# Loading the node features in four pieces instead of two, and running the first layer norm by the same pieces

## The chip, the cores and the metric

The kernel runs on one NeuronCore of a Trainium2 chip, in one launch. The metric is the device time of one execution in microseconds (us); lower is better. Five engines work beside each other, each in the order of its own instruction queue: TensorE (PE) multiplies matrices, VectorE (DVE) does elementwise work and reductions, ScalarE (ACT) applies functions and copies, GpSimd (POOL) does small side work, SyncE (SP) issues transfers. ACT and POOL can issue transfers too. An engine waits for another, or for a transfer, through semaphores.

## What is computed

There are 3327 nodes with 64 features each (`x`) and a dense 3327 x 3327 adjacency matrix (`adj`). Two graph layers follow each other, both of the form "normalise, rectify, aggregate over neighbours, add to x":

```python
def _layernorm(x, axis=-1, eps=1e-5):
    m = jnp.mean(x, axis=axis, keepdims=True)
    v = jnp.var(x, axis=axis, keepdims=True)
    return (x - m) / jnp.sqrt(v + eps)

# --- layer 0: hyperbolic attention over the neighbours ---
h = jnp.maximum(_layernorm(x, axis=-1), 0.0)
x = x + _L0_gnn_ref(h, adj, L0_gnn_r, L0_gnn_w_att, L0_gnn_b_att)
#   left, right = logmap0(h) @ w_att halves
#   adj_att[i,j] = sigmoid(left[i] + right[j] + b) * adj[i,j]
#   support[i]   = sum_j adj_att[i,j] * logmap(h[i], h[j])
#   out          = proj(expmap(h, support))
# --- layer 1: each row's last 100 neighbours, weighted by powers of 1/2 ---
h = jnp.maximum(_layernorm(x, axis=-1), 0.0)
x = x + _L1_gnn_ref(h, adj, L1_gnn_weight, L1_gnn_bias)
```

The change touches only the first layer norm, at the very start: the load of `x`, the row sums, the centred values, their squares and their positive parts.

## The kernel before

The nodes are padded to 3328 = 26 blocks of 128, and a tile holds one node of each block per partition: `x_sb` is 128 partitions x 26 blocks x 64 features, 32-bit. One block of one partition is a run of 256 bytes in memory.

**The opening (lines 452 to 768).** `x_sb` is filled by two transfers of 13 blocks each, the first issued by SP (line 455), the second by ACT (line 456). SP then issues four loads of adjacency tiles (`ad`, line 617, 512 KB each); POOL issues seven small loads, among them `r_c` (line 460) and `w_lr` (line 471), and makes constants. For each half of the blocks, VectorE sums the rows (`m`, line 715) and subtracts the mean (`d`, line 716). ScalarE then forms three tiles: `sq` = d squared (line 717), `rl` = the positive part of d (line 718), `sr` = rl squared (line 719). A second loop over the halves reduces `sq` and `sr` on VectorE to the row quantities `v` and `rs` (lines 721 and 722):

```python
    node_halves = (slice(0, 13), slice(13, NB))
    for hs in node_halves:
        n = hs.stop - hs.start
        V.tensor_reduce(m[:, hs], x_sb[:, hs], AX.X, ALU.add)
        V.scalar_tensor_tensor(d[:, hs], wide(m[:, hs], n), -1.0 / D, x_sb[:, hs], op0=ALU.mult, op1=ALU.add)
        A.activation(sq[:, hs], d[:, hs], AF.Square)
        A.activation(rl[:, hs], d[:, hs], AF.Relu)
        A.activation(sr[:, hs], rl[:, hs], AF.Square)
    for hs in node_halves:
        V.tensor_reduce(v[:, hs], sq[:, hs], AX.X, ALU.add)
        V.tensor_reduce(rs[:, hs], sr[:, hs], AX.X, ALU.add)
```

After `rs` of the second half VectorE runs a long chain of small instructions on all 26 blocks at once (lines 749 to 781): scaling, an inverse square root by Newton steps, and interleaved with it the preparation of constants from `r_c` and `w_lr` (lines 729 to 743; the cast to `w_h` at line 741 needs `w_lr`). ScalarE loads another function table at line 725 and takes logarithms (lines 799 and 800). Then TensorE transposes the features, and the main loop starts.

**The main loop (lines 1194 to 1244).** It goes over four strips of target nodes and over 26 blocks of source nodes; each round loads an `ad` tile, makes a 0/1 `mask` (line 623), counts edges by matmul (lines 634, 635), forms pair products by matmul (lines 673, 674), passes them through ScalarE (lines 1211, 1212, 656) and VectorE (lines 661, 666), and sums by matmul into `po` (line 683). The per-node work of a finished strip is slipped between rounds. Layer 1 follows (lines 1252 to 1327).

**Order.** The instructions of PE, DVE and ACT from line 692 on stand in the order in which the code writes them (`manual_schedule` over these three engines); SP and POOL have queues of their own. A general version of the kernel stands behind a flag and isn't taken for these inputs.

Of the kernel before, what the change touches and what calls it, by code (L numbers as in the profile page):

```python
# [24 lines left out]
NB = 26  # L25
# [420 lines left out]
def fast(ctx, tc, x, adj_t, r, w_att, b_att, weight, bias, out, flag):  # L446

    nc = tc.nc
# [3 lines left out]
    x_sb = const.tile([P, NB, D], F32, name="x_sb")  # L452
    xv = x.rearrange("(t p) d -> p t d", p=P)
    node_halves = (slice(0, 13), slice(13, NB))
    nc.sync.dma_start(x_sb[:, :13], xv[:, :13])
    nc.scalar.dma_start(x_sb[:, 13:], xv[:, 13:])

    def across(src, n, name):
        t = const.tile([P, n], F32, name=name)
# [66 lines left out]
    def wide(t, n):  # L526
        return t[:, :, None].to_broadcast([P, n, D])
# [182 lines left out]
    m, rs = (small(n) for n in ("m", "rs"))  # L710
    v2, y2, t2 = (pre.tile([P, 2, NB], F32, name=n) for n in ("v2", "y2", "t2"))
    v, y = v2[:, 0], y2[:, 0]
    for hs in node_halves:
        n = hs.stop - hs.start
        V.tensor_reduce(m[:, hs], x_sb[:, hs], AX.X, ALU.add)
        V.scalar_tensor_tensor(d[:, hs], wide(m[:, hs], n), -1.0 / D, x_sb[:, hs], op0=ALU.mult, op1=ALU.add)
# [3 lines that stand above are left out]
# [610 lines left out]
@with_exitstack  # L1330
def gnn_kernel(
    ctx: ExitStack,
    tc: tile.TileContext,
    x: bass.AP,
    adj_t: bass.AP,
    r: bass.AP,
    w_att: bass.AP,
    b_att: bass.AP,
    weight: bass.AP,
    bias: bass.AP,  # L1340
    out: bass.AP,
):
    keep = ctx.enter_context(tc.tile_pool(name="keep", bufs=1))
    flag = keep.tile([1, 1], I32, name="flag")
    args = (x, adj_t, r, w_att, b_att, weight, bias, out)
    with ExitStack() as inner:
        fast(inner, tc, *args, flag)
    cond = tc.nc.values_load(flag)
    with tc.If(cond > 0):
        with ExitStack() as inner:  # L1350
            general(inner, tc, *args)
# [28 lines left out]
```

## Time and profile before

| what | value |
|---|---|
| time, median of 8 runs | 419.79 us |
| lowest and highest of the 8 | 417.69 and 421.76 us |
| the profiled execution, its own time | 417.8 us |
| its span, first to last instruction | 415.9 us |
| busy: DVE, ACT, PE, POOL | 91%, 87%, 86%, 27% of the span |
| mean granted TensorE clock | 0.972 of full speed |

The profile is of one execution. Its own time is 1.9 us more than its span, and 2.0 us below the median of the eight runs. All times inside the kernel below are counted from the start of that span. A row of the timeline gives the start, the time taken, the engine, the line, the operation, the tile written and the tiles read, the shape, and in brackets how long the engine had been idle and what ended that. A row of the chain of waits gives a start and a duration on the path that ended last, followed back from the last instruction. A row of the table of stretches gives for each engine its busy time, then the granted clock, the mean busy share of the DMA engines and the GB/s that they moved.

### The profile page before, as it was taken

Reading aid. Unit: us, or ns where it says so; the run is one execution under the profiler, and the core shown is the slowest. Engines: PE = TensorE matmul, PEld = TensorE weight load, DVE = VectorE, ACT = ScalarE, POOL = GpSimd, SP = SyncE. Lnnn points to the kernel's source line nnn. Section 1 sums busy time; section 2 is a strip of 40 time slices with the busy share of each in tenths; the row PEclk is TensorE's granted clock in tenths of the full one; section 3 lists DMA queues with packets and bytes.
Section 4 is the critical chain, followed back from the end, with each engine's and each line's share of the span. In section 5 each row is a group of like instructions: output and inputs, shape, how many; then the busy total and the mean of one; then the engine's idle time right before and its main releaser. Section 6 shows DMA issues by size and latency. Waiting matters only on the chain.

```text
span 415.9 us, 4717 instructions
## 1 busy us (share of the span) xinstructions
PE 359.0 (86%) x1460; PEld 152.9 (37%) x1460; DVE 377.7 (91%) x559; ACT 363.1 (87%) x409; POOL 112.9 (27%) x224
## 2 busy tenths in 40 slices
PE   0085999999997999999999899999787999899793
PEld 0053333333332333333333444444332333344353
DVE  4999999999999989999999998899999899898841
ACT  3587889999998999999999999999996999788820
POOL 7030000000000153950250073810505184452400
PEclk9998899999999899999999999999998999999987
DMA  8313545454548335544445454444543320000012
GB/s 184 157 40 116 178 129 155 134 177 134 176 129 249 102 112 171 154 127 145 139 123 154 122 153 125 141 125 142 172 145 103 110 92 0 2 0 1 2 25 65
DMA packets 23298, 48.99 MB, mean 118 GB/s; under 512 B 8789, under 2 KB 9245, under 8 KB 23265
## 3 DMA queue, kind: packets, MB, share of 16 engines
q1 hardware_dynamic: 20993, 47.66, 37.8%
q0 software_dynamic: 464, 0.49, 0.7%
q10 hardware_dynamic: 1808, 0.46, 0.6%
q8 instruction: 13, 0.21, 0.2%
q14 instruction: 20, 0.16, 0.1%
HBM read 46.40 MB, written 0.87 MB: 114 GB/s over the span
## 4 chain that ended last, share of the span: by engine, by line
DVE 43%; ACT 25%; PE 16%; issue 11%; POOL 3%; DMA 1%; DVEq 0%; POOLq 0%; ACTq 0%
DVE sg L666 12%; DVE sg L661 11%; ACT sg L656 7%; ACT pq L1211 7%; PE po L683 6%; DVE behind_lo L649 3%; DVE wt L1268 3%; ACT pq L1212 3%; DVE behind_hi L649 2%; ACT behind_hi L645 2%; ACT behind_lo L645 2%; PE pq L674 2%; PE pc L634 2%; PE pw L1280 2%; PE pq L673 2%
## 5 line engine op out<-in xcount | busy, mean ns | idle before, releaser
L683 PE MATMUL po<-sg,hw 128*65 128x512 f32 (+1 forms) x364 | 160.7, 565 | 0.4 <-DVE st L958 0.4
L666 DVE SCALAR_TENSOR_TENSOR sg<-pq,sg 128x1024 f32<-128x1024 f32 (+1 forms) x91 | 103.6, 1139 | 6.4 <-ACT pq L1212 5.8
L661 DVE SCALAR_TENSOR_TENSOR sg<-sg,ad 128x1024 f32<-128x1024 f32 (+1 forms) x91 | 103.9, 1142 | 0.1
L656 ACT ACTIVATE sg<-left_b,right 128x1024 f32<-128x1024 f32 (+2 forms) x103 | 99.5, 979 | 0.0
L1211 ACT ACTIVATE pq<-pq 128x1024 f32<-128x1024 f32 (+1 forms) x90 | 86.2, 958 | 2.8 <-PE pq L674 2.7
L1212 ACT ACTIVATE pq<-pq 128x1024 f32<-128x1024 f32 (+1 forms) x90 | 85.3, 947 | 2.9
L683 PEld LDWEIGHTS po<-sg,hw 128*65 128x65 f32 x364 | 49.5, 138 | 70.4 <-issue 56.6
L634 PE MATMUL pc<-mask,ca 128*128 128x512 bf16 (+1 forms) x175 | 64.2, 367 | 12.7 <-DVE behind_hi L649 4.5
L673 PE MATMUL pq<-iu,ju 71*128 71x512 f16 (+1 forms) x182 | 68.4, 376 | 1.4 <-ACT jz L797 0.8
L635 PE MATMUL pc<-mask,cb 128*128 128x512 bf16 (+1 forms) x182 | 65.4, 370 | 2.0 <-ACT behind_lo L645 1.7
L674 PE MATMUL pq<-iz,jz 128*128 128x512 f16 (+1 forms) x182 | 66.8, 374 | 0.0
L623 DVE TENSOR_SCALAR mask<-ad 128x1024 bf16<-128x1024 f32 (+1 forms) x91 | 58.9, 647 | 0.0
L1280 PE MATMUL pw<-wt,s 128*128 128x512 bf16 (+1 forms) x154 | 34.2, 376 | 4.0 <-DVE s L1135 2.2
L635 PEld LDWEIGHTS <-cb 128*128 128x128 bf16 x182 | 17.9, 98 | 53.6 <-issue 42.0
L1030 POOL TENSOR_TENSOR dots<-dots,ih 128x8 f32<-128x8 f32 (+1 forms) x3 | 2.2, 719 | 128.3 <-DVE dots L1050 128.3
L634 PEld LDWEIGHTS <-ca 128*128 128x128 bf16 x175 | 17.1, 98 | 29.6 <-issue 17.7
L1280 PEld LDWEIGHTS <-s 128*128 128x128 f16 x182 | 18.0, 101 | 24.0 <-issue 4.8
L673 PEld LDWEIGHTS <-ju 71*128 71x128 f16 x182 | 18.1, 99 | 23.0 <-DVE sg L666 4.3
L674 PEld LDWEIGHTS <-jz 128*128 128x128 f16 x182 | 18.3, 100 | 19.7 <-issue 2.8
L645 ACT ACTIVATE behind_lo<-pc 128x1024 uint8<-128x1024 f32 (+2 forms) x29 | 24.9, 859 | 0.0
L645 ACT ACTIVATE behind_hi<-pc 128x1024 uint8<-128x1024 f32 (+2 forms) x23 | 19.8, 859 | 5.1 <-PE pc L635 5.0
L1285 POOL TENSOR_TENSOR x_sb<-x_sb,bias_b 128x256 f32<-128x256 f32 (+1 forms) x6 | 9.9, 1657 | 51.3 <-DVE w L1119 45.7
(317 smaller groups left out, 364.5 us busy)
## 6 DMA issues: line engine op xcount, KB each, us to landing
ad<-in_adj_t SPq DMA_DIRECT2D x65, 512.0 KB, 3.5
ad<-in_adj_t SPq DMA_DIRECT2D x26, 384.0 KB, 3.1
out<-o SPq DMA_DIRECT2D x6, 128.0 KB, 1.9
left_b<-left_d SPq DMA_DIRECT2D x1, 512.0 KB, 4.3
x_sb<-in_x ACTq DMA_DIRECT2D x1, 416.0 KB, 5.6
x_sb<-in_x SPq DMA_DIRECT2D x1, 416.0 KB
left_b<-left_d SPq DMA_DIRECT2D x1, 384.0 KB
jz<-iz POOLq DMA_DIRECT2D x2, 128.0 KB, 2.6
```

The source lines that it names most:

```text
L634: T.matmul(S.pc[:, f0:f1], ca, S.before[:, f0:f1], start=False, stop=True, skip_group_check=True)
L635: T.matmul(S.pc[:, f0:f1], cb, now[:, f0:f1], start=S.first, stop=True, skip_group_check=True)
L645: A.activation(kept, S.pc[:, : S.F], AF.Relu, scale=128.0 if j in JD else 1.0)
L656: A.activation(part(n, sg, j), S.left[:, : S.F], AF.Tanh, bias=right[:, j : j + 1], scale=0.5)
L661: V.scalar_tensor_tensor(sg, sg, 1.0, ad_of.pop(n)[:, :w], op0=ALU.add, op1=ALU.mult)
L666: V.scalar_tensor_tensor(sg, pq_of.pop(n)[:, :w], WD, sg, op0=ALU.add, op1=ALU.mult)
L673: T.matmul(part(n, pq, j, f0, f1), ju[:KB, j, :], S.iu[:, f0:f1], start=True, stop=False)
L674: T.matmul(part(n, pq, j, f0, f1), jz[:, j, :], S.iz[:, f0:f1], start=False, stop=True)
L683: T.matmul(S.po[: D + 1, f0:f1], hw[:, j, :], part(n, sg_of[n], j, f0, f1), start=j == NB - 1, stop=j == 0)
L1211: A.activation(pq, pq, AF.Gelu, scale=-WG / QS)
L1212: A.activation(pq, pq, AF.Gelu, scale=WH)
L1280: T.matmul(pw[n], s2[:, j].rearrange("p c d -> p (c d)"), wt[:, f0:f1].bitcast(BF16), start=j == order[0], stop=j == NB - 1)
```

## The change

The two transfers of 13 blocks become four of 7, 6, 7 and 6 blocks: SP issues the first and the third, ACT the second and the fourth. The first loop of the layer norm (`m`, `d`, `sq`, `rl`, `sr`) goes over these four pieces. The second loop (`v`, `rs`) still goes over the two halves; pieces one and two are the first half, three and four the second.

```diff
@@ -452,8 +452,9 @@
     x_sb = const.tile([P, NB, D], F32, name="x_sb")
     xv = x.rearrange("(t p) d -> p t d", p=P)
     node_halves = (slice(0, 13), slice(13, NB))
-    nc.sync.dma_start(x_sb[:, :13], xv[:, :13])
-    nc.scalar.dma_start(x_sb[:, 13:], xv[:, 13:])
+    pieces = (slice(0, 7), slice(7, 13), slice(13, 20), slice(20, NB))
+    for n, part in enumerate(pieces):
+        (nc.scalar if n % 2 else nc.sync).dma_start(x_sb[:, part], xv[:, part])
@@ -710,7 +711,7 @@
     m, rs = (small(n) for n in ("m", "rs"))
     v2, y2, t2 = (pre.tile([P, 2, NB], F32, name=n) for n in ("v2", "y2", "t2"))
     v, y = v2[:, 0], y2[:, 0]
-    for hs in node_halves:
+    for hs in pieces:
         n = hs.stop - hs.start
         V.tensor_reduce(m[:, hs], x_sb[:, hs], AX.X, ALU.add)
         V.scalar_tensor_tensor(d[:, hs], wide(m[:, hs], n), -1.0 / D, x_sb[:, hs], op0=ALU.mult, op1=ALU.add)
```

## The prediction

> **What bounds the kernel now.** I read the page's chain of waits first, then that chain in order of time for the opening, then the timeline of VectorE there, and last the tables of DMA packets and of stretches for the load of x.
>
> The page's shares say what a microsecond is worth, and where:
>
> ```profile
> DVE 43%; ACT 25%; PE 16%; issue 11%; POOL 3%; DMA 1%; DVEq 0%; POOLq 0%; ACTq 0%
> ```
>
> DMA is 1% of the path; it is a single transfer, the first one. The chain for the first 14 us shows it and what comes behind it:
>
> ```profile
> 0.80 4.90 DMA x_sb<-in_x
> 5.72 1.03 DVE m L715
> 6.78 1.17 DVE d L716
> 7.96 0.90 ACT sq L717
> ...
> 10.58 0.79 ACT sq L717
> 11.36 0.80 ACT rl L718
> ...
> 12.18 0.91 ACT sr L719
> ...
> 13.11 1.02 DVE rs L722
> ```
>
> So the path is: wait for the first half of x until 5.70, two VectorE instructions on it, six ScalarE instructions in a row (7.96 to 13.09), then the last reduction at 13.11. From there the whole chain of small instructions hangs on that reduction. I call its start "the mark": whatever moves the mark moves all behind it. VectorE's own timeline shows how close it is to being the bound itself:
>
> ```profile
> 5.72 1.02 DVE L715 TENSOR_REDUCE m<-x_sb 128x13 f32<-128x832 f32 x1 [5.72 <-DMA x_sb<-in_x]
> 7.85 1.01 DVE L715 TENSOR_REDUCE m<-x_sb 128x13 f32<-128x832 f32 x1
> 9.89 1.01 DVE L721 TENSOR_REDUCE v<-sq 128x13 f32<-128x832 f32 x1
> 10.82 1.00 DVE L722 TENSOR_REDUCE rs<-sr 128x13 f32<-128x832 f32 x1
> 11.74 1.00 DVE L721 TENSOR_REDUCE v<-sq 128x13 f32<-128x832 f32 x1
> 13.11 1.02 DVE L722 TENSOR_REDUCE rs<-sr 128x13 f32<-128x832 f32 x1 [0.36 <-ACT sr L719]
> ```
>
> The two pairs m and d take 4.17 us (5.72 to 9.89), the next three reductions step by 0.93 and 0.92, and only 0.36 us of waiting for ScalarE is left before the mark.
>
> **The transfers.** What the SP queue (q1) had moved at 2.7 and at 3.2 us, packets of 256 bytes, and the stretches of one microsecond:
>
> ```profile
> q1 hardware_dynamic: 637, 0.16, 57.8%
> ```
> ```profile
> q1 hardware_dynamic: 1017, 0.26, 66.0%
> ```
> ```profile
> 1.75:2.75 1.00, 0.00 (x0) 0.00 (x0) 0.00 (x0) 0.85 (x1) 0.99 (x3) 1.00 0.76 177
> 2.75:3.75 1.00, 0.00 (x0) 0.00 (x0) 0.00 (x0) 0.00 (x0) 1.00 (x2) 1.00 1.19 271
> ```
>
> A half is 13 x 128 = 1664 packets. SP's half runs alone at first: until 2.7 the ACT queue moved nothing. SP's packets had all run by 4.85, and the wait ended at 5.70, so 0.85 us lie between the last packet and the landing. The ACT half had run by 6.0 and landed at 6.39 (issue at 0.79, 5.6 to landing): 0.4 us.
>
> The first piece of the new kernel is 7 x 128 = 896 packets, issued by the same engine at the same time. Between 637 at 2.7 and 1017 at 3.2 that count is reached at 3.04. With 0.85 to the landing it is there at 3.9, with 0.4 at 3.45. The late bound: ACT's shorter transfer may start earlier beside it, and then half of all bytes (426 kB) are through at 3.67 (177 kB until 2.75, 271 kB in the next microsecond), landing at 4.5. I take 3.9, because SP's own half has the 0.85. VectorE starts at 3.9 instead of 5.7.
>
> **VectorE after it.** Four pairs m and d instead of two. Rows near those sizes: the same two operations on 512 elements take 0.671 and 0.677 (lines 1117 and 1119), on 384 elements 0.543 and 0.558. For 448 elements that is 0.61 and 0.62. Four pairs are 2 x (0.61 + 0.62 + 0.54 + 0.56) = 4.66, less 0.04 overlap each as in the pairs of now: 4.50. The other way: two more reductions at a fixed part of 0.12 (1.014 at 832 against 0.671 at 512) and two more subtractions at 0.20 (0.677 at 512 against 0.558 at 384) on top of 4.17: 4.81. I take 4.65, 0.48 more than now. Then come 2.77 us for v, rs, v, and the mark is 7.42 us after VectorE's start, if neither ScalarE nor a transfer is later.
>
> ScalarE runs twelve instructions instead of six. Independent ones step by 0.51 at 512 elements and 0.20 at 128 (lines 804 to 808), so 0.46 at 448 and 0.41 at 384; `sr` waits some 0.11 more for `rl`, as now. Four pieces are 2 x (1.49 + 1.34) = 5.66, 0.6 more than now. It starts 1.29 after VectorE (0.61 + 0.62 and the gaps), and `sr` is done 7.05 after: 0.37 before VectorE gets to the mark. The 0.6 costs nothing as long as VectorE stays later; if VectorE's four pairs were free of added cost, ScalarE would set the mark at 7.07 instead.
>
> The third piece is needed at about 6.2, the fourth at 7.4. Today both halves have landed by 6.39, and the bytes are the same, so I charge no wait.
>
> **Sum.** The mark moves from 13.11 to 3.9 + 7.42 = 11.32: 1.8 us earlier. Bounds: 3.45 + 7.27 = 10.72 (2.4 earlier), 4.5 + 7.58 = 12.08 (1.0 earlier).
>
> [...]
>
> **What else moves.** SP's second issue (0.44) and ACT's (0.49) come ahead of the `ad` loads and of ScalarE's table load (1.32 to 2.60). ScalarE's first instruction comes at 5.2, so the table load is covered with 2 us to spare. The first `mask` needs its `ad` at 22.72, now 20.9; 0.44 us more is covered by more than ten. On POOL's queue the second `w_lr` was issued at 4.34 and took at most 9.2, so it is there by 13.5; the cast at line 741 needs it at 16.07, now 14.3. That cover falls from 2.5 to 0.8 us, and what it lacks beyond that VectorE would wait. Behind the mark all waits are between engines, so I let the shift pass to the end in full. The one thing with a time of its own may be TensorE's clock: its mean grant is 0.87 from 21 to 46 us and 0.99 from 46 to 365. Where these slow stretches fall against the work I bound at 0.5 us either way.
>
> The profiled execution would take 417.8 - 1.8 = 416.0. It stood 2.0 below the median; against the median I forecast 419.8 - 1.8 = 418.0. The eight runs lie 4.1 us apart, and I estimate from that a scatter of about 1 us between two medians; 0.5%, 2.1 us, is about what a measurement of this kernel can tell from no change.
>
> **The rivals.**
>
> *The landing stays where it is.* If the four transfers interleave so that none is complete before about 5.7, VectorE starts at 5.72 and the mark comes at 13.14: 419.8, no change. For it: both queues feed the same 16 engines, busy at 1.19 to 1.35 in the table of stretches from 2.75 to 5.75. Against it: SP's packets run alone first. 5%.
>
> *More than the sum.* First piece at 3.45 and the cheaper pairs: 2.4 earlier, with up to 0.5 from the clock, 417.0. 14%.
>
> *The adjacency tiles get in ahead of the fourth piece.* ACT's second transfer is issued at about 1.3, beside SP's first `ad` load, whose packets are 4 KB against 256 bytes. If those take the engines first, VectorE stands at the fourth `m` with the reductions of the first half queued behind it, though their data are ready. From that landing to the mark it is 0.54 + 0.56 + 2.77 = 3.9 us: a landing after 9.2 makes the kernel slower, after 11.3 by over 0.5%. Four tiles are 2.1 MB, at the 274 GB/s of 5.72 to 13.11 some 7.7 us; landing behind all of them, at about 14, gives 17.9 and 424.6. Against it: ACT's half ran out today while the first `ad` began, and ACT's part shrinks from 13 to 12 blocks, SP's grows to 14. 7%.
>
> **How the numbers follow.** The forecast case (1.0 to 2.4 us less) has 74%; at 1.8 and the scatter of 1 us about 0.30 of that falls beyond 2.1 us, 0.42 within 0.5%, 0.02 on the slow side. The larger gain adds 0.13 to faster and 0.01 to within. No earlier landing adds 0.03 to within and 0.02 to slower. The tiles in front add 0.07 to slower. Together 0.43, 0.46, 0.11. The likeliest case gives 417.4 to 418.8 before scatter; with it, and with the case of no change at the upper end, 416.5 to 420.3.
>
> **What would show it.** Right: the first `m` starts between 3.5 and 4.5 on 448 elements; four pairs in 4.5 to 4.8 us; no idle time before the third and fourth `m`; `rs` of the second half at 10.7 to 12.1 with no wait for `sr`; the transposes of line 831, now at 21.09, at 19 to 20; the same distance from there to the end of the span. Wrong: a first `m` after 5; an idle time on DMA before a later `m`; a wait at line 741; or a shift at line 831 that is gone by the end.

## The result and the profile after

The changed kernel is slower: 422.12 us median of 22 runs (419.43 to 426.77), against 419.49 us median of 64 runs of the kernel before. The ratio is 1.0068, with a 95% interval of 1.0051 to 1.0085. The forecast was 418.0, in a range of 416.5 to 420.3.

The profiled execution of the changed kernel took 426.17 us with a span of 424.4; it is one of the longest, and the ratio leaves such runs out (the means of all 22 and all 64 runs have the ratio 1.0073). A second profiled execution of the same kernel is shown further down. I call the start of the last `rs` reduction the mark, as the prediction does; it was at 13.11 before.

In the page after, the shares of the chain and the issues of x:

```profile
DVE 40%; ACT 23%; PE 18%; issue 11%; DMA 3%; POOL 2%; ACTq 0%; DVEq 0%; POOLq 0%
...
x_sb<-in_x SPq DMA_DIRECT2D x2, 224.0 KB, 3.6
x_sb<-in_x ACTq DMA_DIRECT2D x2, 192.0 KB, 9.4
```

DMA went from 1% of the path to 3%. The last number of an issue's line is the median time to landing: 3.6 us on SP's queue and 9.4 on ACT's (the middle between its two pieces, 4.0 and 14.7), where half of x needed 5.6 before. The chain of waits in order of time says which transfer it is:

```profile
0.80 0.51 ACTq L457
...
1.33 14.74 DMA x_sb<-in_x
...
16.10 0.56 DVE m L716
...
16.68 0.56 DVE d L717
```

The path now runs through ACT's second issue, the fourth piece. It was issued at 1.33 and landed at 16.07. VectorE's timeline (start, time taken, then idle time before in brackets) has the rest:

```profile
4.42 0.62 DVE L716 TENSOR_REDUCE m<-x_sb 128x7 f32<-128x448 f32 x1 [4.42 <-DMA x_sb<-in_x]
...
6.20 1.27 DVE L717 SCALAR_TENSOR_TENSOR d<-m,x_sb 128x384 f32<-128x384 f32 x1
7.39 0.60 DVE L716 TENSOR_REDUCE m<-x_sb 128x7 f32<-128x448 f32 x1
8.03 0.62 DVE L717 SCALAR_TENSOR_TENSOR d<-m,x_sb 128x448 f32<-128x448 f32 x1
16.10 0.55 DVE L716 TENSOR_REDUCE m<-x_sb 128x6 f32<-128x384 f32 x1 [7.44 <-DMA x_sb<-in_x]
...
19.94 1.01 DVE L723 TENSOR_REDUCE rs<-sr 128x13 f32<-128x832 f32 x1
```

The first piece is early, as forecast (4.42 instead of 5.72). Three pieces are done by 8.65. Then VectorE stands for 7.44 us at the fourth `m`, and the mark is at 19.94, 3.84 us behind that `m`. What the queues moved between 6.5 and 15 us (packets, MB, share of 16 engines' time):

```profile
q1 hardware_dynamic: 625, 2.27, 66.4%
q0 software_dynamic: 203, 0.07, 16.2%
q10 hardware_dynamic: 122, 0.03, 1.6%
```

q10 is ACT's queue. Of the 768 packets of 256 bytes of the fourth piece, 114 were still under way in this stretch (the other 8 of the 122 have 4 bytes), beside 625 packets of SP's adjacency loads (q1) and 203 of GpSimd's small loads (q0). In the kernel before, ACT's queue moved nothing in the same stretch. So two candidates stand beside the late piece, and the experiments part them.

### The profile page after: what moved, and what is told of

It reads as the page before. It is cut to its first block, busy times and chain, and to the rows that moved or that the text cites. A ratio compares the mean times of both kernels' runs of the same rounds, so it can differ in the third digit from the quotient of the medians.

```text
span 424.4 us, 4730 instructions
## 1 busy us (share of the span) xinstructions
PE 360.5 (85%) x1460; PEld 154.6 (36%) x1460; DVE 378.8 (89%) x563; ACT 364.1 (86%) x415; POOL 111.8 (26%) x224
## 4 chain that ended last, share of the span: by engine, by line
DVE 40%; ACT 23%; PE 18%; issue 11%; DMA 3%; POOL 2%; ACTq 0%; DVEq 0%; POOLq 0%
DVE sg L667 11%; DVE sg L662 10%; ACT sg L657 7%; ACT pq L1212 7%; PE po L684 6%; DMA x_sb<-in_x 3%; DVE behind_lo L650 3%; DVE wt L1269 3%; ACT pq L1213 3%; PE pq L675 2%; PE pq L674 2%; PE pc L636 2%; PE pc L635 2%; ACT behind_hi L646 2%; ACT behind_lo L646 2%
## 5 line engine op out<-in xcount | busy, mean ns | idle before, releaser
L832 PE MATMUL pq<-id,nui 128*71 128x128 f16 x8 | 1.0, 308 | 27.9 <-ACT nzi L806 27.9
```

## The experiments

**The theories.** A: the adjacency packets of SP's queue, 4 KB each, take the engines from the last packets of ACT's queue. B: GpSimd's seven small loads, while in flight, hold up whatever of x is left. C: four transfers have a fixed cost each. D: the smaller instructions cost the time.

All kernels in one view. Landings are from the trace's records of transfers, the mark and the first transpose (line 831 of the kernel before) from each run's timeline; the medians are of 10 to 12 runs, beside 419.45 to 419.62 for the kernel before on the same chips (22 and 64 runs in the first two rows). The ratio isn't the quotient of the two medians and can differ from it by up to 0.3%; how sure a difference is, its interval says. Landings, mark and first transpose are of one execution each.

| kernel | third, fourth piece landed | mark | first transpose | median us | ratio to before (95%) |
|---|---|---|---|---|---|
| before (halves) | 5.70, 6.40 | 13.11 | 21.09 | 419.49 | |
| changed, first profile | 5.88, 16.07 | 19.94 | 27.90 | 422.12 | 1.0068 (1.0051 to 1.0085) |
| changed, second profile | 7.46, 8.91 | 12.78 | 20.74 | 421.87 | 1.0065 (1.0035 to 1.0095) |
| e1, transfers only | 6.20, 13.40 | 18.20 | 26.16 | 423.43 | 1.0063 (1.0030 to 1.0096) |
| e2, instructions only | 5.59, 6.39 (halves) | 13.55 | 21.52 | 420.18 | 1.0022 (1.0000 to 1.0043) |
| e3, all pieces on SP | 8.14, 11.42 | 15.29 | 23.25 | 421.55 | 1.0057 (1.0035 to 1.0079) |
| e4, most adjacency loads held | 6.16, 9.77 | 13.63 | 21.60 | 420.14 | 0.9994 (0.9971 to 1.0017) |
| e5, small loads held | 6.10, 9.42 | 13.29 | 22.44 | 419.85 | 1.0017 (0.9995 to 1.0038) |
| e6, all on SP, small loads held | 5.96, 6.64 | 11.22 | 20.78 | 418.88 | 0.9991 (0.9975 to 1.0006) |
| e7, adjacency loads held | 6.05, 7.83 | 12.42 | 20.39 | 418.71 | 0.9984 (0.9965 to 1.0002) |
| e8, both held | 6.00, 6.41 | 11.62 | 20.32 | 418.71 | 0.9991 (0.9972 to 1.0009) |
| e9, small loads by SP | 6.05, 6.51 | 11.72 | 19.70 | 418.02 | 0.9961 (0.9940 to 0.9981) |
| e10, pieces and small loads by SP | 5.80, 6.41 | 11.06 | 19.03 | 417.59 | 0.9958 (0.9936 to 0.9979) |
| e11, before, small loads by SP | 5.95, 6.45 (halves) | 13.23 | 21.20 | 419.39 | 1.0001 (0.9978 to 1.0024) |

**One part alone, e1 and e2.** e1 keeps the four transfers and runs the layer norm by halves:

```diff
-    for hs in pieces:
+    for hs in node_halves:
```

> Four transfers as in the changed kernel, the layer norm by halves as in the kernel before. Theory (the last piece, on ACT's queue, loses the engines to the adjacency loads that SP's queue holds behind its own pieces): the fourth piece lands spread between about 9 and 17 us, the second m waits for it, the last rs starts 4.9 us after that landing, and the time is 1.5 to 5 us over the kernel before, as slow as the changed kernel or up to 1 us slower. Rival (twelve smaller vector and scalar instructions cost the time): within 0.5 us of the kernel before, since none of them is there.

e2 keeps the two transfers and runs the layer norm by the four pieces:

```diff
-    for n, part in enumerate(pieces):
-        (nc.scalar if n % 2 else nc.sync).dma_start(x_sb[:, part], xv[:, part])
+    nc.sync.dma_start(x_sb[:, :13], xv[:, :13])
+    nc.scalar.dma_start(x_sb[:, 13:], xv[:, 13:])
```

> Two transfers as in the kernel before, the layer norm by the four pieces. Theory (late last piece): both halves land by 6.4, no wait before any m but the first, the last rs at about 13.1, the time within 0.7 us of the kernel before. Rival (smaller instructions cost the time): 2 to 3 us slower, the last rs at 15 or later.

The transfers alone give the whole loss (ratio 1.0063 beside 1.0068, the fourth piece at 13.40). The instructions alone give 420.18, 0.7 us over the kernel before, with the mark 0.44 later: D is out as the cause of the loss. The interval of e2 touches 1, so its 0.7 isn't sure.

**Nothing ahead of the fourth piece, e3.**

```diff
-    for n, part in enumerate(pieces):
-        (nc.scalar if n % 2 else nc.sync).dma_start(x_sb[:, part], xv[:, part])
+    for part in pieces:
+        nc.sync.dma_start(x_sb[:, part], xv[:, part])
```

> All four pieces issued by SP, ahead of the adjacency loads in the same queue; ACT issues none. Theory (last piece passed by the adjacency packets of the other queue): nothing can pass it; SP's queue alone moved some 760 packets of 256 bytes per us, so the pieces land at about 3.9, 4.9, 6.0 and 7.1, the last rs starts at 11.3 to 11.8, and the time is 1.0 to 2.0 us below the kernel before. Rival (four transfers have a fixed cost each, whatever is beside them): gaps of 0.5 us or more between the pieces, the fourth after 8.5, the time equal to the kernel before or slower.

Theory A failed here as the only cause, and what was expected for C came true. All four pieces stand in one queue ahead of the adjacency loads, and still VectorE waited twice:

```profile
8.16 0.62 DVE L716 TENSOR_REDUCE m<-x_sb 128x7 f32<-128x448 f32 x1 [1.96 <-DMA x_sb<-in_x]
...
11.44 0.55 DVE L716 TENSOR_REDUCE m<-x_sb 128x6 f32<-128x384 f32 x1 [1.97 <-DMA x_sb<-in_x]
```

From 4.5 to 7.5 us the queues of e3 moved this (packets, MB, share of 16 engines):

```profile
q1 hardware_dynamic: 897, 0.23, 33.3%
q0 software_dynamic: 54, 0.02, 21.0%
```

897 packets took 33.3% of 16 x 3 us, 18 ns each; 54 packets of the small loads took 21.0%. That is 0.19 us on average, but the average hides two kinds: 43 packets of 4 or 32 bytes took 9 to 15 ns each, and eleven of 2 KB took 0.87 us each. The engines weren't full: x trickled. It did so before the first 2 KB packet ran (6.09): from 3.5 to 6.0 us the small loads' 50 packets took 1.5% of the engines, and x moved 1103 packets, where e6 below, without small loads, moved 1930 on that queue, nearly all of x. That suggested theory B, which I had not had.

**The adjacency loads held, e4.**

```diff
         ad_of[n] = ad = work.tile([P, FMAX], F32, name="ad", bufs=ADB)
+        if n < LOADS:
+            G.tensor_copy(ad[:, :1], x_sb[:, NB - 1, :1])
```

> As the changed kernel, but the first four adjacency loads are issued only when the fourth piece has landed (GpSimd copies one column of it into each tile first). Theory (passed by the adjacency packets): the fourth piece lands by 6.6, the last rs starts at 11.3 to 12.0, and the time is 1.0 to 2.0 us below the kernel before; the first mask still finds its tile. Rival (fixed cost of each transfer): the fourth piece is as late as in the changed kernel, 9 to 16 us, and the time 2 us or more above the kernel before.

This run was less clean than meant: the fifth load, whose tile wasn't held, was issued ahead of the four held ones, at 1.88. With this one load and the small loads beside it the fourth piece landed at 9.77, within what was expected for the rival, but the time is within noise of the kernel before (0.9994) and not 2 us over it: neither expectation was met.

**Each suspect held by itself, and both, e5 to e8.** In e5 the small loads wait for the fourth piece, in e7 all of the first five adjacency loads do, in e8 both; e6 is e3 with the small loads held.

```diff
# e5, e6, e8
     def across(src, n, name):
         t = const.tile([P, n], F32, name=name)
+        G.tensor_copy(t[:, :1], x_sb[:, NB - 1, :1])
...
     for half in (slice(0, D), slice(D, P)):
+        G.tensor_copy(w_lr[half, :1], x_sb[half, NB - 1, :1])
+        G.tensor_copy(w2[half, :1], x_sb[half, NB - 1, :1])
# e7, e8
+        if n <= LOADS:
+            G.tensor_copy(ad[:, :1], x_sb[:, NB - 1, :1])
```

> As the changed kernel, but GpSimd's seven small loads (r_c, batt, bias_b, w_lr, w2) are issued only when the fourth piece has landed. Theory A (the adjacency packets of SP's queue pass the last piece): no help, the fourth piece still lands at 9 to 16 us and the time stays 1.5 us or more above the kernel before. Theory B (while the small loads of GpSimd's queue are in flight, the 16 engines trickle, and whatever of x is then left is held up; that would explain the all-on-SP run, where nothing stood ahead of the fourth piece): the fourth piece lands by 7, the last rs starts at 11.3 to 12.2, the time is 1 to 2 us below the kernel before. If w_lr is late at its cast, that shows as a wait there.

> All four pieces on SP as in the run before, GpSimd's seven small loads held until the fourth has landed. Theory A or a fixed cost of each transfer: the third and fourth piece stay late, 8.1 and 11.4 as in the run with the small loads free. Theory B (small loads hold the engines up): the pieces land at about 3.9, 4.6, 6.0 and 7.1, the last rs starts at 11.4 to 12.2, the time is 1 to 2 us below the kernel before.

> As the changed kernel, but all of the first five adjacency loads wait for the fourth piece (in the earlier run one of them, for a tile that was not held, was issued ahead); the small loads are free. Theory A (adjacency packets pass): the fourth piece lands by 6.8, the time is 0.5 to 1.5 us below the kernel before (less than the sum of the forecast, since the second subtraction took 0.7 us longer). Theory B (small loads): the fourth piece lands at 8 to 10 without any adjacency packet beside it, the time within 0.7 us of the kernel before.

> As the changed kernel, with both the small loads and the first five adjacency loads held until the fourth piece has landed. Both theories: all four pieces by 6.8 and the last rs at 11.2 to 12. If the pieces are late here too, both theories fall, and the four transfers themselves are slow. The time is 1 to 2 us below the kernel before, unless w_lr or the first adjacency tiles now come too late, which shows as a wait at the cast or at the first mask.

The last transfer of x to land, measured from its issue at 1.33 (the line gives the least, the median and the longest of the transfers that the view could time): e5 and e7, each with one suspect left, then e8 with none.

```profile
DMA to landing us min/median/max: 3.6/4.1/8.1
```
```profile
DMA to landing us min/median/max: 3.6/4.0/6.5
```
```profile
DMA to landing us min/median/max: 3.5/4.0/5.1
```

With neither the fourth piece is there at 6.41. The adjacency packets alone make that 9.42 (3.0 later), the small loads alone 7.83 (1.4 later). Both together gave 8.91 and 16.07 in the two profiles of the changed kernel and 13.40 in e1: up to 9.7 later, more than the sum of the two in two of three executions. So A and B both hold. In e5 and e7 neither expectation was met as it stood, since each had reckoned with one cause alone. The sizes 3.0 and 1.4 are of one execution each, and the landing varies from one execution to the next; that either cause delays the fourth piece is surer than by how much. C is out: in e8 four transfers have all landed at the moment when two had. e6 says the same for one queue: with the small loads held, the third and fourth piece came at 5.96 and 6.64 instead of 8.14 and 11.42, and q1 (the rest of x and the first adjacency packets) moved in the stretch from 4.5 to 7.5

```profile
q1 hardware_dynamic: 1184, 0.88, 115.2%
```

with no small load beside it (over 100%, since the times of packets overlap).

In e6 the mark came at 11.22, 1.9 us before that of the kernel before, and yet the time fell by only 0.74, with an interval that takes in 1. The timeline shows where the rest went:

```profile
11.22 1.02 DVE L726 TENSOR_REDUCE rs<-sr 128x13 f32<-128x832 f32 x1
13.59 0.16 DVE L733 RECIPROCAL inv_r<-r_c 128x1 f32<-128x1 f32 x1 [0.16 <-DMA r_c<-in_r]
15.81 0.17 DVE L745 CAST w_h<-w_lr 128x2 f16<-128x2 f32 x1 [1.11 <-DMA w_lr<-in_w_att]
```

Holding the small loads made `r_c` and `w_lr` late: 1.27 us of new waits behind the mark. From the mark to the first transpose e6 needs 9.56 us, where before it was 7.98. e5 (9.15) and e8 (8.70) lose there too; e7, whose small loads are free, does not (7.97), and its time fell by 0.9 with a mark 0.7 earlier (its interval just takes in 1). The medians of e5 don't fit as well: a first transpose 1.35 later, and only 0.2 us more time. One profile beside twelve runs can't settle that.

**Both causes taken away without holding anything, e9 to e11.** SP issues the small loads itself, behind its pieces and ahead of the adjacency loads; GpSimd issues none. e9 is the changed kernel with that edit, e10 the one with all pieces on SP, e11 the kernel before. The edit changes three things at once: the queue of the small loads; the order, since the first small load lands behind the last of x and the first adjacency load is issued only at 7.04 (e9), 7.70 (e10) and 6.97 (e11), where the changed kernel issues it at 1.89; and the packets, since in these traces no small load by SP has one of over 256 bytes. So these runs show an order that works, and not which of the three matters.

```diff
-        nc.gpsimd.dma_start(t, bass.AP(tensor=src.tensor, offset=src.offset, ap=[[0, P], [1, n]]))
+        nc.sync.dma_start(t, bass.AP(tensor=src.tensor, offset=src.offset, ap=[[0, P], [1, n]]))
...
-        nc.gpsimd.dma_start(w_lr[half], bass.AP(tensor=w_att.tensor, offset=w_att.offset, ap=[[1, D], [D, 2]]))
-        nc.gpsimd.dma_start(w2[half], weight)
+        nc.sync.dma_start(w_lr[half], bass.AP(tensor=w_att.tensor, offset=w_att.offset, ap=[[1, D], [D, 2]]))
+        nc.sync.dma_start(w2[half], weight)
```

> As the changed kernel, but the seven small loads are issued by SP, behind its two pieces and ahead of the adjacency loads; GpSimd issues none of them. If both causes hold (small loads in GpSimd's queue, adjacency packets beside the last piece): all four pieces by 6.8, the second subtraction at 0.6 and not 1.3, the last rs at 11.4 to 12, r_c and w_lr there without a wait, and the time 1.0 to 2.0 us below the kernel before. If it is the small loads as such, in whatever queue, the fourth piece on ACT's queue lands after 7.5 and the last rs starts after 12.5.

> All four pieces on SP, behind them the seven small loads, behind these the adjacency loads, all in SP's queue. If both causes hold: pieces at 3.9, 4.8, 6.0 and 6.7 as with the small loads held, the last rs at 11.2 to 11.5, no wait for r_c or w_lr (there these two waits gave back 1.3 us), and the time 1.3 to 2.2 us below the kernel before. Rival (a shift at the start is lost later, whatever its cause): the last rs as early, the time within 0.7 us of the kernel before.

> The kernel before (two transfers, halves) with the seven small loads issued by SP instead of GpSimd. Both halves by 6.4, the last rs at about 13.1, the time within 0.7 us of the kernel before: moving the small loads alone brings nothing, since the halves of x were never held up by them. If it is 1 us or more faster, the gain of the two kernels beside it is not the four pieces' own.

e10 is the fastest of all: 417.59, ratio 0.9958 (0.9936 to 0.9979) to the kernel before, and its interval lies wholly below that of the changed kernel. No piece is waited for after the first:

```profile
3.77 0.62 DVE L716 TENSOR_REDUCE m<-x_sb 128x7 f32<-128x448 f32 x1 [3.77 <-DMA x_sb<-in_x]
...
8.26 1.01 DVE L722 TENSOR_REDUCE v<-sq 128x13 f32<-128x832 f32 x1
...
11.06 1.02 DVE L723 TENSOR_REDUCE rs<-sr 128x13 f32<-128x832 f32 x1
```

e11 shows that moving the small loads alone brings nothing (mark 13.23, 419.39). So against e11 the four pieces bring 2.2 us at the mark and 1.8 us in time, when nothing holds them up. The rival of e10 (a shift at the start is lost later) is out: mark 2.05 earlier than before, first transpose 2.06 earlier, time 1.96 less.

**The changed kernel again, e12,** unaltered.

> The changed kernel once more, unaltered, for a second profile: the runs of it lie from 419.4 to 426.8, and the profile shown is near the upper end. If the landing of the fourth piece sets the time, this execution has another landing (between 8 and 16 us), the last rs starts 3.85 us after it, and its span differs from the first profile's by about the difference of the landings, within 1.5 us for TensorE's clock. If the span differs while the landing is the same, something else spreads the runs.

```profile
8.93 0.55 DVE L716 TENSOR_REDUCE m<-x_sb 128x6 f32<-128x384 f32 x1 [0.17 <-DMA x_sb<-in_x]
...
12.78 1.01 DVE L723 TENSOR_REDUCE rs<-sr 128x13 f32<-128x832 f32 x1
```

The same program, another landing: 8.91 instead of 16.07, a mark 7.16 earlier, a span of 415.2 instead of 424.4 and a time of 416.88, faster than the median of the kernel before. The last `rs` starts 3.85 after that `m`, as expected. So the landing makes most of the difference between these two executions; that it spreads all the runs is inferred from them. The spans differ by 9.2, the landings by 7.16; that is 2.0 more, where I had allowed 1.5. TensorE's mean granted clock from 20 to 60 us was 0.87 in the first and 0.91 in the second, 1.6 us of full speed over these 40 us. That would fit, but no run took the clock apart from the landing.

## Why the prediction was wrong, step by step

**The step that failed** is the one on the later pieces: "Today both halves have landed by 6.39, and the bytes are the same, so I charge no wait." The bytes were the same, but not what stood beside them. With nothing beside it the fourth piece landed at 6.41 (e8); beside the adjacency loads, the small loads or both it landed at 7.83 to 16.07, and in the first profile VectorE stood 7.44 us at the fourth `m`. The kernel before had nearly all of x through when the small loads and the adjacency loads took up speed (their first packets ran at 5.29 and 5.31 us): from 5.5 us on ACT's queue had 75 packets left to move, in the changed kernel 273. There ACT's queue sagged between its two transfers: 569 packets from 2.5 to 3.5 us, but from 4.0 to 4.5

```profile
q1 hardware_dynamic: 368, 0.09, 113.6%
q10 hardware_dynamic: 66, 0.02, 20.3%
```

while SP's second piece ran on. So the tail of the fourth piece fell into the time of the other loads, and there it waited up to 9.7 us. The sag alone costs nothing: e8 has it too (65 packets from 4.0 to 4.5). Why ACT's queue sags there no run shows.

**The rival that came true had 7%.** "The adjacency tiles get in ahead of the fourth piece" named the place, the queue and the wait rightly, and its price of 3.9 us from the landing to the mark was measured at 3.87. Its break-even, a landing at 9.2, holds too: 8.91 gave a mark of 12.78, before 13.11, and 9.42 (e5) one of 13.29, behind it. What spoke against it, that SP's share grows from 13 to 14 blocks and ACT's shrinks, was a count of packets and not of when they run. The small loads as a second cause were missed, although the packet counts of the kernel before had them in q0: between 6.5 and 15 us 204 packets of 0.07 MB took

```profile
q0 software_dynamic: 204, 0.07, 15.4%
```

of 16 engines, nearly all of it in sixteen packets of 2 KB, 1.11 us each (32 KB in all, the size of `bias_b`).

**The other steps.** The first landing, forecast at 3.9 within 3.45 to 4.5, was 4.40, 1.30 before the half of the kernel before: ACT's shorter transfer did run beside it from early on (569 packets on its queue from 2.5 to 3.5 us, 533 on SP's). On SP alone, where nothing did, it was 3.74 to 3.90 (e3, e6, e10). The four pairs took 4.49 us in e10 (3.77 to 8.26), at the lower of my two bounds (4.50 and 4.81), and the way from VectorE's start to the mark 7.29 instead of 7.42. The mark of 11.32 is where it came when nothing held the pieces up: 11.06 to 11.72 in e6, e8, e9 and e10. The four added instructions cost 0.32 (4.49 against 4.17), where I had taken 0.48. ScalarE never set the mark: no `rs` waited for `sr` in any kernel by pieces. The sum for it has a slip (1.29 + 5.66 is 6.95, not 7.05), on which nothing hung. That the shift passes to the end in full was right (e9, e10). The clock, bounded at 0.5 us, was sized too small if the 2.0 us above are its doing.

**An unforeseen term in the pairs.** The second subtraction took 1.27 us in the changed kernel, not 0.56. GpSimd ran its constants just then:

```profile
6.21 0.35 POOL L495 TENSOR_SCALAR_AFFINE_SELECT cb<-ca 128x128 bf16<-128x128 bf16 x1
6.46 0.34 POOL L490 CAST id<-ident 128x128 f16<-128x128 f32 x1
6.71 0.34 POOL L497 TENSOR_SCALAR_AFFINE_SELECT cb<-cb 128x128 bf16<-128x128 bf16 x1
```

In e5, where GpSimd stands still from 6 to 7.5 us, the same subtraction at the same time took

```profile
6.19 0.56 DVE L720 SCALAR_TENSOR_TENSOR d<-m,x_sb 128x384 f32<-128x384 f32 x1
```

The reductions beside GpSimd's work kept their time (0.55). In e2 it was the first subtraction that met this work, 1.27 us on 448 elements instead of 0.62; that 0.65 is more than the whole 0.44 by which e2's mark is late. Begun at 6.12 to 6.17, the second subtraction took 1.34 in the second profile, 1.33 in e4 and 1.30 in e7. The subtraction reads two tiles (`m`, `x_sb`), the reduction one (1.27 against 0.55 here). But in e1, where GpSimd has the same code, a subtraction of 832 elements begun at 5.87 took 1.02, and one at 14.48 took 1.03. What slows it no run shows.

## What to carry to other kernels

A transfer cut in pieces gains only if its last piece still lands in time: with the fourth at 6.41 the mark came 2.05 us earlier than before (e10), with it at 16.07 it came 6.83 later (first profile). Look at what else is in flight when that piece runs, not at the sum of the bytes. Here the fourth piece, in packets of 256 bytes, landed at 9.42 beside packets of 4 KB of another queue (e5), at 7.83 beside the seven tiny loads (e7) and at 6.41 beside neither (e8); putting the pieces first, the tiny loads behind them and the bulk last into one queue had it there at 6.41 too (e10). If the runs of one kernel spread by 7 us where those of its predecessor spread by 4.5, look for a landing time that varies.

## What the hardware showed beyond that

- Seven small loads issued by GpSimd slowed the transfers of other queues: with all of x in SP's queue the fourth piece landed at 11.42 with them and at 6.64 without. The same loads issued by SP behind x didn't (6.41 in e10). It isn't the engines' time that they take: from 3.5 to 6.0 us in e3 their packets took 1.5% of it, and x moved at little over half the rate of e6. How the one holds up the other isn't shown.
- In the first profile of the changed kernel the trace records sixteen landings for the fourth piece, from 5.87 to 16.07: twelve of them by 7.62, the last two at 13.65 and 16.07. VectorE's wait for that piece ended at 16.10, behind the last.
- From 6.5 to 15 us of the first profile a 4 KB packet of the adjacency loads took 0.16 us, one of x 18 ns. The last twelve packets of x end from 13.78 to 15.49, in ten of the eleven steps 0.17 us apart, and none ends from 8.63 to 9.80 or from 11.01 to 12.15. If a packet of x had to wait for one adjacency packet, that would give the steps, and a wait for one 2 KB packet of the small loads (1.18 us on average) each of the gaps. That is my estimate from these times; which engine ran which packet isn't recorded, so it is argued and not shown.
